# Page buffers, the last pages, transposes and one-hot matrices in a fused graph and expert kernel

## The chip, the cores and the metric

The kernel runs on one NeuronCore of a Trainium2 chip. Its five engines each work through a queue of their own in order: TensorE (PE, with its weight loads PEld), VectorE (DVE), ScalarE (ACT), GpSimd (POOL) and SyncE (SP, which here only issues DMAs). They meet through semaphores. The metric is the device time of one execution in microseconds (us), as the median of several runs.

## The reference, cut to what matters

```python
x = x + agg(layernorm(x)) @ W.T + b          # 12500 nodes, 256 features
#   agg: msgs = features[src] * edge_weight  # 212500 edges, sorted by dst
#        segment_sum(msgs, dst)
h = layernorm(x)
p = softmax(h @ gate_w + gate_b)             # 8 experts
e = argmax(p); pos = rank of the token among the tokens of e, in order
y = relu(h @ w1[e] + b1[e]) @ w2[e] + b2[e]  # 256 -> 1024 -> 256
y = y * p[e] if pos < 1954 else 0            # capacity of an expert
x = x + nan_to_num(y)
```

All of it is float32. One in seventeen of the edges is a node's own loop, the others are random, so the sum over neighbours needs one gathered row of 1 KB for each edge.

## The kernel before, in words

**Edges.** The 212500 edges are cut into 1661 blocks of 128. For a block `k`, `gather(k)` (line 597) is one indirect DMA on POOL that brings 128 rows into the tile `m`; `onehot(k)` (line 605) is one VectorE instruction that makes a 128x128 matrix `h` whose row is the edge's weight at the column of its target; `product(k)` (line 611) multiplies the two on TensorE into the PSUM tile `pw`. Fifteen blocks make a group, after which ScalarE copies `pw` to `ws` (line 619). The pool of `m` has 32 buffers, that of `h` has 12.

**Prologue.** `table()` (line 752) writes the normalised features to `feat` in DRAM, in 14 chunks of eight tiles. Meanwhile the first 112 blocks are gathered from `x` itself and normalised through their weights. In one turn `i` of its loop ScalarE takes statistics of four of the blocks that were gathered (`junk`, lines 772 and 775), scales a chunk (`xn`, line 788), stores it (line 790) and takes a root (`sd`). VectorE takes the other statistics, makes `wr` (line 811) and then, for the eight blocks of turn `i - 2`, one one-hot matrix and one product each (lines 812 to 814). The gathers after the prologue read `feat`, so the first of them waits for the last store.

**Main loop.** From then on one loop (line 826) writes down the order of all engines, step by step: one gather, one scatter or one piece of a page's end, one-hot matrices until `made` is eight blocks ahead of `done` (lines 837 to 839), one product that lies sixteen blocks behind the gather, a piece of `nodes()`, a piece of `experts()`. No scheduler moves anything afterwards.

**Nodes and routing.** `nodes()` (line 622) adds the groups up for each tile of 128 nodes, multiplies by `W`, and for each chunk of eight tiles `route()` (line 244) finds the expert and the place of each token. Its rows go by indirect DMA from POOL (`put`, line 339) to `buf` in DRAM, which holds a page of 128 tokens for each 128 places of an expert. `listing()` (line 360) then finds which pages have become full and writes their numbers to `li`; `SLOTS` (line 49) says how many are taken after each chunk, as pairs of pages at first and as single pages after the last three.

**Pages.** `load()` (line 427) reads a page's number into a register of SP and issues five DMAs there: the page `pg` (line 437), `b1_sb`, `b2_sb`, and the weights `w1_sb` and `w2_sb` of 1 MB each (lines 448 and 450). `pg` has two buffers, the four others have three. `fresh()` (line 454) normalises on VectorE to `xg`, `turn()` (line 461) transposes on TensorE and copies with ScalarE to `gT`, `products()` (line 472) multiplies by `w1` into `ph` (line 481), applies the bias and relu on ScalarE (line 485), and multiplies by `w2` into `py` (line 492). `finish()` (line 498) adds `b2_sb` (line 502), scales on ScalarE (line 505), cleans infinities and adds the page's rows (lines 509 to 518), takes the token numbers out of `pg` (`tok`, line 520), and sends the rows to `out` by indirect DMA on POOL (line 523). `tok` is the last reader of `pg`. In the main loop `experts()` (line 678) holds up to two loaded pages in `ready`, starts a page `LOADED` (20) steps after its load, and spreads it by `PACE`.

**The last pages.** After the loop, `rest()` (line 544) finds the page of each expert that is only partly full (`last()`, line 410), loads and multiplies these eight in a row, with the transposes of the next page between the two products (`between`, line 556), and lists what was left over; here nothing was. A second way of summing the edges (line 860 on) is there for inputs that the first can't hold; with these inputs it isn't entered.

Of the kernel before, what the change touches and what calls it, by code (L numbers as in the profile page):

```python
# [9 lines left out]
F32 = mybir.dt.float32  # L10
# [8 lines left out]
P = 128  # L19
N = 12500  # L20
D = 256
E = 8
# [20 lines left out]
RW = D + 4  # L43
# [8 lines left out]
LEFT = 24  # L52


LEAD = 16
AHEAD = 8
LOADED = 20
PACE = {1: 2.3, 2: 3.0}

# [2 lines left out]
RB = 8  # L62
# [6 lines left out]
KT = (NE + P - 1) // P  # L69
# [23 lines left out]
def gnn_moe_kernel(ctx: ExitStack, tc: tile.TileContext, x, src, dst, ew, wT, gb, gate_w, gate_b,  # L93
# [123 lines left out]
    class Ffn:  # L217
# [209 lines left out]
        def load(self, of, li, i, e=None):  # L427
            p4 = self.p4
            at = li[0:1, 0, i:i + 1] if e is None else li[0:1, e:e + 1]
            row = nc.values_load(at, engines=[mybir.EngineType.SP], min_val=0, max_val=NP_ * P,  # L430
                                 skip_runtime_bounds_check_because="a page, or the empty one")
            if e is None:
                e = nc.values_load(li[0:1, 1, i:i + 1], engines=[mybir.EngineType.SP], min_val=0,
                                   max_val=E - 1,
                                   skip_runtime_bounds_check_because="an expert")
            pg = p4.tile([P, 2, RW], F32, name="pg")
            self.loads.append(nc.sync.dma_start(
                pg[:, :of, :], buf[ds(row, of * P), :].rearrange("(a p) d -> p a d", p=P)))
            return (of, pg) + self.weights(e)
# [95 lines left out]
                send(a)  # L535
                yield 1

        def page(self, of, li, i):
            got = self.load(of, li, i)
            through(self.products(*got, self.turn(got[0], self.fresh(*got[:2]))))  # L540
            through(self.out)


        def rest(self):
            lp = self.last()
            got, turned = {}, {}
            for e in range(2):
                got[e] = self.load(1, lp, 0, e)
            through(self.listing(1, LEFT, count=True))
            news = {0: self.fresh(*got[0][:2])}  # L550
            turned[0] = self.turn(1, news[0])
            for e in range(E):
                if e + 2 < E:
                    got[e + 2] = self.load(1, lp, 0, e + 2)

                def between():
                    if e + 1 < E:
                        turned[e + 1] = self.turn(1, news[e + 1])

                if e + 1 < E:  # L560
                    news[e + 1] = self.fresh(*got[e + 1][:2])
                through(self.products(*got[e], turned[e], between))
                through(self.out)
            left = nc.values_load(left_i, min_val=0, max_val=LEFT,  # L564
                                  skip_runtime_bounds_check_because="a count of pages")
            with tc.If(left > 0):
                self.sends, self.before = [], None
                for i in range(4):
                    self.page(1, self.li, i)
                with tc.If(left > 4):  # L570
                    self.sends = []
                    for i in range(4, LEFT):
                        self.page(1, self.li, i)


    with tc.tile_pool(name="edges", bufs=1) as edges:
# [8 lines left out]
        with tc.tile_pool(name="p2", bufs=32) as p2, tc.tile_pool(name="p2h", bufs=12) as p2h, \  # L585
# [9 lines left out]
            pool_q, pages = [], []  # L595
# [26 lines left out]
            def nodes():  # L622
                xs, shifts = [], {}

                def shift(t):

                    for g in groups_of(t) if t < NT else ():
                        s = p2o.tile([P, P], F32, name="s", bufs=8)
                        nc.vector.tensor_scalar(s, cols, float(P * t), win[:, g:g + 1], op0=ALU.add,  # L629
                                                op1=ALU.is_equal)  # L630
                        shifts[t, g] = s

                for c, (t0, nt, rows) in enumerate(CHUNKS):
                    rt = p3.tile([P, CH, RW], F32, name="rt")
                    ln = ln_new(p3)
                    for t in range(t0, t0 + nt):
                        for i in range(len(xs), min(t + 3, NT)):
                            x_ = p3.tile([P, D], F32, name="xt", bufs=4)
                            r = min(P, N - i * P)
                            nc.scalar.dma_start(x_[:r, :], x[i * P:i * P + r, :])  # L640
                            xs.append(x_)
                        if t == 0:
                            shift(t)
                        gs = groups_of(t)
                        while gs[-1] not in sums:
# [12 lines left out]
                        yield  # L658
                        px = ffn.psum("px")[:, :D]
                        for k in range(2):  # L660
                            nc.tensor.matmul(px[:rows, :], aT[:, k * P:k * P + rows], wT_sb[:, k, :],  # L661
                                             start=(k == 0), stop=(k == 1))
                        x1 = rt[:rows, t - t0, :D]
                        nc.vector.tensor_add(x1, xs[t][:rows, :], px[:rows, :])  # L664
                        nc.vector.tensor_add(x1, x1, gb_sb[:rows, :])
                        ln_stats(ln, x1, t - t0, rows)
                    yield from ffn.route(rt, ln, t0, nt, rows)
                    pool_q.extend(ffn.put)
                    if c < len(CHUNKS) - 1 and SLOTS[c][1]:
                        yield from ffn.listing(*SLOTS[c])  # L670
                        li = ffn.li
                        while pool_q:
                            yield
                        of, n = SLOTS[c]
                        pages.extend((of, li, i) for i in range(n))
                        yield

            def experts(now):
                ready, work, at = [], None, 0.0
                while pages or ready or work:  # L680
                    if pages and len(ready) < 2:
                        ready.append([now[0], ffn.load(*pages.pop(0)), None])
                    if ready and not ready[0][2] and now[0] >= ready[0][0] + LOADED - 3:
                        ready[0][2] = ffn.fresh(*ready[0][1][:2])
                    if not work and ready and now[0] >= max(at, ready[0][0] + LOADED):
                        _, got, xg = ready.pop(0)
                        at = max(at, now[0]) + PACE[got[0]]
                        work = ffn.products(*got, ffn.turn(got[0], xg))
                    elif work and now[0] >= at:
                        at += PACE[got[0]]  # L690
                        if next(work, None) is None:
                            work = None
                            outs.append(ffn.out)
                    yield
# [57 lines left out]
            def table():  # L752
# [3 lines left out]
                for i in range(n + 2):  # L756
# [51 lines left out]
                    if i >= 2:  # L808
                        k0 = (i - 2) * RB
                        wr = p3.tile([P, RB], F32, name="wr")  # L810
                        nc.vector.tensor_mul(wr, w_sb[:, k0:k0 + RB], r[:, CH:])
                        for k in range(k0, k0 + RB):
                            onehot(k, wr[:, k - k0:k - k0 + 1])
# [12 lines left out]
            while alive or pages or b or outs:  # L826
# [33 lines left out]
    with tc.If(some > 0):  # L860
# [49 lines left out]
        with tc.tile_pool(name="q3", bufs=2) as p3, tc.tile_pool(name="q4", bufs=2) as p4, \  # L910
# [6 lines left out]
            for c, (t0, nt, rows) in enumerate(CHUNKS):  # L917
# [25 lines left out]
                if c < len(CHUNKS) - 1 and SLOTS[c][1]:  # L943
                    through(ffn.listing(*SLOTS[c]))
                    for i in range(SLOTS[c][1]):
                        ffn.page(SLOTS[c][0], ffn.li, i)
            ffn.rest()


# [38 lines left out]
```

## Time and profile before

| | us |
|---|---|
| median of 3 runs (2605.55 to 2607.30) | 2607.29 |
| the profiled execution, its own time | 2604.47 |
| its span, first to last instruction | 2602.7 |
| PE, DVE, ACT, POOL busy | 2038.7, 1156.7, 503.9, 1809.1 |
| mean granted clock of TensorE | 0.856 of full |
| gathers from `feat` on POOL, 1549 | 1511.3 busy, 976 ns each |
| DMA | 455.67 MB, 175 GB/s over the span |

Busy time isn't the same as what sets the end: for a stage one looks at which engine waits for nothing there. A line of the timeline has the start, the duration, engine, source line, operation, `output<-inputs`, a count of neighbours of the same kind (x8), and in brackets the idle time of that engine just ahead and what ended it. A line of a table of stretches has, after the length, each engine's busy us and number of instructions, then the granted clock, the busy share of the 16 DMA engines and their GB/s. "SPq" is SP's queue of DMA issues.

### The profile page before, as it was taken

Reading aid. Unit: us, or ns where it says so; the run is one execution under the profiler, and the core shown is the slowest. Engines: PE = TensorE matmul, PEld = TensorE weight load, DVE = VectorE, ACT = ScalarE, POOL = GpSimd, SP = SyncE. Lnnn points to the kernel's source line nnn. Section 1 sums busy time; section 2 is a strip of 40 time slices with the busy share of each in tenths; the row PEclk is TensorE's granted clock in tenths of the full one; section 3 lists DMA queues with packets and bytes.
Section 4 is the critical chain, followed back from the end, with each engine's and each line's share of the span. In section 5 each row is a group of like instructions: output and inputs, shape, how many; then the busy total and the mean of one; then the engine's idle time right before and its main releaser. Section 6 shows DMA issues by size and latency. Waiting matters only on the chain. (4 is left out here: it accounts for less than half of the span.)

```text
span 2602.7 us, 31144 instructions
## 1 busy us (share of the span) xinstructions
PE 2038.7 (78%) x9082; PEld 1619.6 (62%) x9082; DVE 1156.7 (44%) x4287; ACT 503.9 (19%) x1315; POOL 1809.1 (70%) x1859
## 2 busy tenths in 40 slices
PE   2568778887788788788788788788888787788765
PEld 2456545674677576576676676676676565577764
DVE  6875434345336236235335335335335344354322
ACT  5751001111112112112112112112111111122322
POOL 7657777777777777777777777777777777774100
PEclk9668777899789799799889888899898897899978
DMA  8869334544564564564654654654653534677765
GB/s 280 282 205 330 115 107 124 188 150 125 188 185 123 185 186 122 187 184 121 190 182 121 190 183 120 188 182 120 188 183 118 186 109 124 205 246 224 218 185 153
DMA packets 264704, 455.67 MB, mean 175 GB/s; under 512 B 44799, under 2 KB 190406, under 8 KB 264520
## 3 DMA queue, kind: packets, MB, share of 16 engines
q0 software_dynamic: 88800, 240.41, 30.3%
q1 hardware_dynamic: 136210, 174.68, 21.3%
q10 hardware_dynamic: 39510, 38.41, 4.5%
q8 instruction: 81, 1.33, 0.2%
q14 instruction: 103, 0.84, 0.1%
HBM read 387.86 MB, written 67.83 MB: 175 GB/s over the span
## 5 line engine op out<-in xcount | busy, mean ns | idle before, releaser
L599 POOL DMA_INDIRECT m<-feat,src_i x1549 | 1511.3, 976 | 491.0 <-issue 222.4
L616 PE MATMUL pw<-m,h 128*128 128x256 f32 x3322 | 1104.1, 450 | 421.3 <-DMA m<-feat,src_i 294.8
L616 PEld LDWEIGHTS pw<-m,h 128*128 128x128 f32 x3322 | 663.1, 221 | 681.5 <-issue 267.7
L607 DVE TENSOR_SCALAR h<-cols,rel,w_sb 128x128 f32<-128x128 f32 x1549 | 470.4, 357 | 296.6 <-PE pw L616 293.5
L481 PE MATMUL ph<-gT,w_sb 128*128 128x256 f32 (+1 forms) x1856 | 374.6, 355 | 30.7 <-DMA w_sb<-in_w 23.8
L481 PEld LDWEIGHTS ph<-gT,w_sb 128*128 128x128 f32 x1856 | 319.0, 206 | 69.8 <-issue 27.1
L492 PE MATMUL py<-w_sb,hT 128*128 128x256 f32 x1456 | 348.3, 384 | 0.0
L492 PEld LDWEIGHTS py<-w_sb,hT 128*128 128x128 f32 x1456 | 277.1, 193 | 36.6
L485 ACT ACTIVATE hT<-ph,b_sb 128x256 f32<-128x256 f32 (+1 forms) x464 | 168.0, 426 | 510.1 <-PE ph L481 482.2
L523 POOL DMA_INDIRECT out<-z,tok x91 | 90.8, 998 | 189.5 <-DVE tok L520 140.4
L664 DVE TENSOR_TENSOR rt<-xt,ms 128x256 f32<-128x256 f32 x98 | 41.0, 419 | 335.7 <-PE ms L661 335.6
L652 PEld LDWEIGHTS ms<-s,ws 128*128 128x128 f32 x1116 | 175.4, 214 | 18.2 <-DVE s L629 3.1
L652 PE MATMUL ms<-s,ws 128*128 128x128 f32 x1116 | 174.9, 297 | 3.3 <-DVE s L629 3.3
L457 DVE TENSOR_SCALAR xg<-pg 128x256 f32<-128x256 f32 x91 | 35.9, 424 | 298.5 <-DMA pg<-buf 298.5
L619 ACT COPY ws<-pw 128x256 f32<-128x256 f32 x111 | 41.2, 371 | 615.2 <-PE pw L616 615.1
L502 DVE TENSOR_TENSOR y<-py,b_sb 128x512 f32<-128x512 f32 (+1 forms) x58 | 33.4, 576 | 242.8 <-PE py L492 242.8
L599 POOL DMA_INDIRECT m<-in_x,src_i x112 | 107.5, 960 | 46.5 <-issue 22.6
L339 POOL DMA_INDIRECT buf<-rt,to x98 | 98.4, 1004 | 51.7 <-issue 18.6
L661 PE MATMUL ms<-wT_sb,aT 128*128 128x256 f32 x392 | 106.5, 396 | 2.5 <-ACT aT L656 2.4
L505 ACT ACTIVATE y<-y,pg 128x256 f32<-128x256 f32 x91 | 42.7, 503 | 314.0 <-DVE y L502 255.7
L656 ACT COPY aT<-ms 128x256 f32<-128x256 f32 x98 | 36.6, 373 | 261.8 <-PE ms L652 259.5
L661 PEld LDWEIGHTS ms<-wT_sb,aT 128*128 128x128 f32 x392 | 77.3, 199 | 15.4 <-ACT aT L656 4.1
(159 smaller groups left out, 1255.5 us busy)
## 6 DMA issues: line engine op xcount, KB each, us to landing
w_sb<-in_w SPq DMA_DIRECT2D x116, 1024.0 KB, 10.7
m<-feat,src_i POOLq DMA_INDIRECT x1549, 2.8
buf<-fill SPq DMA_DIRECT2D x13, 1300.0 KB
xt<-in_x ACTq DMA_DIRECT2D x97, 128.0 KB, 2.3
xt<-in_x SPq DMA_DIRECT2D x12, 1024.0 KB
feat<-xn ACTq DMA_DIRECT2D x12, 1024.0 KB, 10.6
out<-rt ACTq DMA_DIRECT2D x11, 1024.0 KB, 4.8
pg<-buf SPq DMA_DIRECT2D x33, 260.0 KB, 3.0
```

The source lines that it names most:

```text
L339: s = nc.gpsimd.indirect_dma_start(out=buf[:, :], out_offset=bass.IndirectOffsetOnAxis(ap=to[:, j, :], axis=0), in_=rt[:rows, j, :], in_of ...
L481: nc.tensor.matmul(ph[:, c:c + n], w1_sb[:, k, f * P:(f + 1) * P], xT[:, k * n:(k + 1) * n], start=(k == 0), stop=(k == 1))
L485: nc.scalar.activation(hT[:, f, :n], ph[:, c:c + n], AF.Relu, bias=b1_sb[:, f:f + 1])
L492: nc.tensor.matmul(py[:, a, :], hT[:, f, a * P:(a + 1) * P], w2_sb[:, f, :], start=(f == 0), stop=(f == F // P - 1))
L505: nc.scalar.activation(y[:, a, :], y[:, a, :], AF.Copy, scale=pg[:, a, D + 2:D + 3])
L523: s = nc.gpsimd.indirect_dma_start(out=out[:, :], out_offset=bass.IndirectOffsetOnAxis(ap=to[:, a, :], axis=0), in_=z[:, a, :], in_offset= ...
L599: nc.gpsimd.indirect_dma_start(out=m, out_offset=None, in_=x[:, :] if k < RAW else feat[:, :], in_offset=bass.IndirectOffsetOnAxis(ap=src_ ...
L607: nc.vector.tensor_scalar(h, cols, rel[:, k:k + 1], w_sb[:, k:k + 1] if w is None else w, op0=ALU.is_equal, op1=ALU.mult)
L616: nc.tensor.matmul(product.pw, hs.pop(k), ms.pop(k), start=(j == 0), stop=last)
L619: nc.scalar.copy(ws, product.pw)
L652: nc.tensor.matmul(pa[:, k * P:(k + 1) * P], sums[g][:, k * P:(k + 1) * P], shifts[t, g], start=(g == gs[0]), stop=(g == gs[-1]))
L661: nc.tensor.matmul(px[:rows, :], aT[:, k * P:k * P + rows], wT_sb[:, k, :], start=(k == 0), stop=(k == 1))
```

## The change

Five things are edited. `pg` gets four buffers. `rest()` keeps only the pages that are left over: the eight partly full pages are now found by `nodes()` after the last chunk, with `last()` and the last `listing()`, and join the queue that `experts()` works off. `experts()` keeps a page's transposed rows beside it in `ready`, and hands `between` to `products()`, so that the transposes of the next page, if its `xg` is made, are issued between the two products of the one at work. In the prologue the eight one-hot matrices of a turn are made in reversed order, all ahead of the eight products. In the main loop they are made four at a time (`HB`), in reversed order, when the number that is ahead falls below eight. The other way of summing edges gets the same last pages.

```diff
+HB = 4
@@ load
-            pg = p4.tile([P, 2, RW], F32, name="pg")
+            pg = p4.tile([P, 2, RW], F32, name="pg", bufs=4)
@@ rest
-            lp = self.last()
-            got, turned = {}, {}
-            for e in range(2):
-                got[e] = self.load(1, lp, 0, e)
-            through(self.listing(1, LEFT, count=True))
...
-                through(self.products(*got[e], turned[e], between))
-                through(self.out)
             left = nc.values_load(left_i, min_val=0, max_val=LEFT,
@@ nodes
                     pool_q.extend(ffn.put)
-                    if c < len(CHUNKS) - 1 and SLOTS[c][1]:
-                        yield from ffn.listing(*SLOTS[c])
+                    last = c == len(CHUNKS) - 1
+                    if last or SLOTS[c][1]:
+                        if last:
+                            lp = ffn.last()
+                        yield from ffn.listing(*SLOTS[c] if not last else (1, LEFT, True))
                         li = ffn.li
                         while pool_q:
                             yield
-                        of, n = SLOTS[c]
-                        pages.extend((of, li, i) for i in range(n))
+                        if last:
+                            pages.extend((1, lp, 0, e) for e in range(E))
+                        else:
+                            of, n = SLOTS[c]
+                            pages.extend((of, li, i) for i in range(n))
                         yield
@@ experts
                 ready, work, at = [], None, 0.0
+
+
+                def between():
+                    if ready and ready[0][2] and not ready[0][3]:
+                        ready[0][3] = ffn.turn(ready[0][1][0], ready[0][2])
+
                 while pages or ready or work:
                     if pages and len(ready) < 2:
-                        ready.append([now[0], ffn.load(*pages.pop(0)), None])
+                        ready.append([now[0], ffn.load(*pages.pop(0)), None, None])
...
-                        _, got, xg = ready.pop(0)
+                        _, got, xg, xT = ready.pop(0)
                         at = max(at, now[0]) + PACE[got[0]]
-                        work = ffn.products(*got, ffn.turn(got[0], xg))
+                        work = ffn.products(*got, xT or ffn.turn(got[0], xg), between)
@@ table
-                        for k in range(k0, k0 + RB):
+                        for k in reversed(range(k0, k0 + RB)):
                             onehot(k, wr[:, k - k0:k - k0 + 1])
+                        for k in range(k0, k0 + RB):
                             product(k)
@@ main loop
-                while made < min(KT, max(done, s - LEAD) + AHEAD):
-                    onehot(made)
-                    made += 1
+                if made < min(KT, max(done, s - LEAD) + AHEAD):
+                    for k in reversed(range(made, min(KT, made + HB))):
+                        onehot(k)
+                    made = min(KT, made + HB)
```

More of the change, by code (lines that the diff above doesn't have):

```diff
@@ L536, in finish, with page @@
                 yield 1
-        def page(self, of, li, i):
-            got = self.load(of, li, i)
+        def page(self, *what):
+            got = self.load(*what)
             through(self.products(*got, self.turn(got[0], self.fresh(*got[:2]))))
@@ L544, in rest @@
         def rest(self):
-            lp = self.last()
-            got, turned = {}, {}
-            for e in range(2):
-                got[e] = self.load(1, lp, 0, e)
-            through(self.listing(1, LEFT, count=True))
[L550 to L561, printed above, removed]
-                through(self.products(*got[e], turned[e], between))
-                through(self.out)
             left = nc.values_load(left_i, min_val=0, max_val=LEFT,
@@ L811, in table @@
                         nc.vector.tensor_mul(wr, w_sb[:, k0:k0 + RB], r[:, CH:])
+                        for k in reversed(range(k0, k0 + RB)):
+                            onehot(k, wr[:, k - k0:k - k0 + 1])
                         for k in range(k0, k0 + RB):
-                            onehot(k, wr[:, k - k0:k - k0 + 1])
                             product(k)
@@ L946, in gnn_moe_kernel @@
                         ffn.page(SLOTS[c][0], ffn.li, i)
+            through(ffn.listing(1, LEFT, count=True))
+            lp = ffn.last()
+            for e in range(E):
+                ffn.page(1, lp, 0, e)
             ffn.rest()
```

## The prediction

> **What bounds the kernel now.** I read the busy time by slices first, then cut the span where POOL's behaviour changes, and read each stretch from its timeline.
>
> ```profile
> 0.00:172.70 172.70, 80.39 (x214) 61.09 (x214) 130.27 (x564) 115.89 (x346) 108.69 (x121) 0.78 0.77 251
> 172.70:2374.10 2201.40, 1798.79 (x7896) 1415.73 (x7895) 954.83 (x3446) 325.55 (x779) 1677.04 (x1714) 0.86 0.54 168
> 2374.10:2490.00 115.90, 93.00 (x567) 83.28 (x565) 44.20 (x182) 37.60 (x111) 14.65 (x16) 0.93 0.64 202
> 2490.00:2602.70 112.70, 66.54 (x410) 59.46 (x410) 27.41 (x97) 24.90 (x80) 8.75 (x9) 0.85 0.58 175
> ```
>
> Row 2 is the main loop. POOL's timeline there shows a gather of 0.95 us, 0.30 us of gap and the next gather, 1.25 us a step. From 188 us to the last gather at 2373.17 only one gap is over 0.35 us (0.82, at 1265.83). The loop is therefore POOL's, whatever PE (82% busy) does. Gather k waits for product k-32, issued 16 steps earlier, so PE may fall some 16 steps (20 us) behind before POOL notices.
>
> Row 1, the prologue, ends with the first gather from `feat`:
>
> ```profile
> 143.63 2.14 DVE L607 TENSOR_SCALAR h<-cols,rel,wr 128x128 f32<-128x128 f32 x8
> 144.03 4.21 PE L616 MATMUL pw<-m,h 128*128 128x256 f32 x9 [4.84 <-DVE h L607]
> 144.41 0.22 ACT L183 ACTIVATE sd<-ve 128x16 f32<-128x16 f32 x1 [0.47 <-DVE h L607]
> 146.99 0.37 ACT L619 COPY ws<-pw 128x256 f32<-128x256 f32 x1 [2.36 <-PE pw L616]
> ...
> 172.72 0.94 POOL L599 DMA_INDIRECT m<-feat,src_i  x1 [16.97 <-PE pw L616]
> ```
>
> PE starts when the first of eight one-hot matrices is made; ACT, in order, stands before `ws` until PE has closed a group. The gather at 172.72 names PE, but that product was long done: the last store of `feat` was issued at 168.99, behind ACT's work. Turns without a `ws` copy take ACT 9.24 us (`sd` at 41.42, then 50.66), with no idle time; a turn with one takes that plus the wait (6.20, then 15.8). VectorE in turn waits for `sd` (2.0 to 2.2 us) after most such copies. The chain ACT, DVE, PE, ACT sets the prologue.
>
> Rows 3 and 4, the tail, hold 17 single pages. From PE's timeline, and then DVE's and SP's:
>
> ```profile
> 2477.27 6.72 PE L481 MATMUL ph<-gT,w_sb 128*128 128x128 f32 x32 [3.21 <-DMA w_sb<-in_w]
> 2483.83 3.62 PE L492 MATMUL py<-w_sb,hT 128*128 128x256 f32 x16
> 2492.00 0.20 PE L422 MATMUL ms<-c,page_of 128*1 128x8 f32 x2 [4.54 <-DVE c L420]
> ...
> 2502.05 6.30 PE L481 MATMUL ph<-gT,w_sb 128*128 128x128 f32 x32 [4.49 <-DMA w_sb<-in_w]
> 2508.19 0.38 PE L466 MATMUL pT<-ident,xg 128*128 128x128 f32 x2
> 2508.40 3.62 PE L492 MATMUL py<-w_sb,hT 128*128 128x256 f32 x16
> 2511.86 3.73 PE L481 MATMUL ph<-gT,w_sb 128*128 128x128 f32 x32
> ```
>
> ```profile
> 2515.13 0.15 DVE L520 CAST tok<-pg 128x1 int32<-128x1 f32 x1
> ...
> 2515.41 0.36 SPq L437 DMA_DIRECT2D pg<-buf  x1
> ```
>
> ```profile
> SPq L437 <- DVE tok L520: 720.3, 35, 37.5
> ```
>
> PE waits for weights; the weights are issued 1.4 to 1.9 us after `pg` in SP's order; and `pg`, with two buffers, waits until `tok` of two pages earlier is read. So a load starts only as the page ahead of it starts its first product.
>
> **The Trainium skill.** "DMA: Bandwidth & Descriptors", Anatomy of one DMA: semaphore waits are made by the issuing sequencer, not by the DMA engines; the lines above agree (0.13 us from the end of `tok` to the issue, the weights queued behind). The same page, Specifications, gives some 358 GB/s of HBM for a core; single microseconds of the tail show 382 and 391 GB/s. "TensorE: Matmul & The Clock Gate", Part 1: an idle PE drops to half clock and warms up again; the trace agrees (32 matmuls 3.73 us warm, 6.30 and 6.72 after idling). "SBUF — State Buffer", Who interferes with whom: a VectorE instruction in a two-port mode locks GpSimd out for its length. Partly seen: the gather at 1223.37 took 3.02 us under the unbroken `fin`, `hi`, `z` of a page, and six such gathers cost 11.9 us over 0.95 each; but 60 gathers wholly under one-hot matrices averaged 0.976, against 0.953 for 554 with VectorE idle.
>
> **The change, part by part**, against the span of 2602.7.
>
> *One-hot matrices in the prologue.* PE's first product now waits for the last of eight matrices: 7 x 0.267 (2.14/8) = 1.87 us later. Six `ws` copies lie ahead of the last store (waits 6.20, 4.73, 4.36, 3.13, 2.36, 1.35), none hidden: 6 x 1.87 = **+11.2**. Bound below: 0, if the chain has slack. Above 13.1, a seventh. PE loses seven of eight semaphore waits a burst; I give that nothing, since the bursts are paced by PE's clock.
>
> *One-hot matrices in fours.* The number is the same; DVE now waits on a product two steps behind instead of five, and what stands behind it there (node sums, `xn`, `xg`) may be up to 1.1 us later; its readers on PE come two steps, 2.5 us, later. Covered by POOL. Without the cover, it is 4 x 0.27 = 1.07 us per four steps of PE. **0.**
>
> *Four `pg` buffers in the loop.* The third load of a chunk follows the second at once (weights have three buffers), so about 21 us of full DMA instead of 14, beside the gathers. Before, ten such bursts gave one POOL stall of 0.82. I take **+3**; bounds 0 and +12 (1 us a burst). The meeting of gathers with page ends can shift too: -12 (none of the six) to +54 (all 33 pairs, 27 more at 2 us).
>
> *Transposes between products.* In the tail PE idled for `gT` up to 2.3 us a page; now its copy lies under the second product. In the loop it is nothing (POOL).
>
> *The last pages, and `pg` in the tail.* A load is now held by `b2_sb` (three buffers, free at the y addition of the previous page), 15 us ahead of its use, against some 8 us for 2.37 MB (30.64 MB at 63.3% of 160 us for 13 pages is 7.8 us each of DMA). So PE should set the pitch: 3.83 (product to transposes, at 2556.03) + 0.25 + 3.46 (2508.40 to 2511.86) = 7.54; `xg` follows `finish` of the page before (y addition 2512.06, `tok` done 2515.28, `xg` 0.41), ready about when PE asks: 7.65, against 10.1 before.
> Start: `last()` now stands in PE's order before the fourth tail page. DVE had `to` of the last chunk at 2429.05; its six small instructions take 1.34, so `L424` runs at about 2430.5 and that page starts at 2430.7 instead of 2426.87. PE has idled 6.2 us, and I add 2.7 for the cold clock (6.3 and 6.72 against 3.8) and 0.6 for the listing: next page at 2441.7. Then 13 x 7.65 = 99.5: the last product ends at 2541.1 against 2583.9, **-42.8**. What follows (3.5 us of finish, one send, the end) stays. The 14.6 us hole around 2492 is in this sum. SP's extra wait, for `lp`, is over two pages before its first load is due.
>
> Sum: +11.2 + 3 - 42.8 = -28.6, a span of 2574 and a median of 2607.3 - 28.6 = **2578.7**, 1.1% less. The profiled execution lies 2.8 below the median shown, so 0.1% goes with which run one takes; under 0.2% can't be told from no change.
>
> **Rivals.**
> (B) *The prologue hides it.* If ACT or DVE has slack that the waits don't show, the +11.2 goes: 2567.5. For it: DVE idles 1 to 2 us before `ve` in some turns. Against: ACT doesn't idle otherwise.
> (C) *Weights set the tail.* Two loads overlapping, with the slow row of `b2_sb` (79 and 94 GB/s at 80 to 92% busy for 2 us), may need 9.0 us: 13 x 1.35 = +17.5, 2596. Against: full streams reach 380 GB/s.
> (D) *Slower.* Fours put unbroken VectorE work ahead of `fin`, `hi`, `z`, and more gathers are locked out for 2 us. From 14 more on, of 27 possible pairs, the gain is gone; all 27 give 2633. For it: all six cases had four one-hot matrices just ahead. Against: `fin` waits for ACT's y, which usually opens a gap.
> (E) *The loads stay late* because another wait on SP replaces `pg`: the pitch stays at 10.1, 13 x 2.45 = 31.9 of the gain are lost, 2610.6.
>
> **How the numbers follow.** A 0.55 (own range 2568 to 2588), B 0.17, C 0.14, D 0.08, E 0.06. Leaving out D, E and some 0.05 at the low end gives 2560 to 2600. Faster: A, B, C, 0.86. Same: most of E and a little of D, 0.06. Slower: 0.08.
>
> **What would show it.** Right: first `feat` gather near 184 us; `ws` waits 1.9 longer; gathers still 1.25 apart; last gather near 2387; PE in the tail at 7.6 to 7.8 a page with no wait for weights, a 6 us hole before `last()`'s matmul. Wrong: a first gather at 173 (B), waits for `w_sb` in the tail (C, E), many gathers of 3 us (D).

## The result, and the profile after

| us | before | after |
|---|---|---|
| median | 2607.3 (2605.55 to 2610.18, 4 runs) | 2575.53 (2568.71 to 2578.96, 4 runs) |
| profiled execution, its span | 2604.47, 2602.7 | 2575.36, 2573.6 |
| mean granted clock of TensorE | 0.856 | 0.867 |

The ratio is 0.9874, with a 95% interval of 0.9852 to 0.9896: the change takes 1.3% off. Two later comparisons put it 29.0 and 31.1 us below the kernel before (changed_third and changed_again, among the experiments). The forecast was 2578.7, 3.2 us above the median, and the case with the greatest chance came. Three of its terms were off all the same, and they cancelled. I cut both spans at two events that each kernel has: the first gather from `feat`, and the start of the last full product of a node step (`ms<-wT_sb,aT`, 128x256).

| stretch, us | before | after | difference | forecast |
|---|---|---|---|---|
| prologue, to the first `feat` gather | 172.72 | 182.48 | +9.76 | +11.2 |
| loop, to the last full node product | 2211.29 | 2204.70 | -6.59 | +3 |
| tail, from there to the end | 218.69 | 186.42 | -32.27 | -42.8 |
| span | 2602.7 | 2573.6 | -29.1 | -28.6 |

Of the loop's 6.59 us, 4.37 lie between the first and the last `feat` gather (2200.45 us before, 2196.08 after); the other 2.22 come off what lies between POOL's last gather and the last full node product (10.84 before, 8.62 after).

The table of stretches of the kernel after (columns as in the prediction; the cuts are the first and the last `feat` gather and the start of the even pages):

```profile
0.00:182.48 182.48, 75.57 (x201) 57.49 (x202) 130.55 (x564) 115.79 (x345) 109.26 (x121) 0.77 0.73 238
182.48:2378.56 2196.08, 1815.94 (x7921) 1402.36 (x7920) 977.23 (x3450) 326.63 (x779) 1671.78 (x1713) 0.87 0.54 170
2378.56:2457.00 78.44, 58.36 (x316) 51.01 (x315) 30.57 (x150) 22.45 (x61) 10.74 (x11) 0.83 0.48 155
2457.00:2573.60 116.60, 96.50 (x650) 88.82 (x648) 38.67 (x124) 40.00 (x130) 13.63 (x14) 0.94 0.73 234
```

VectorE, ACT and POOL did the same work as before in the prologue (130.27, 115.89 and 108.69 us busy then) and had 10 us more for it. In the third row PE is busy 74% of the time at a clock of 0.83; in the fourth, 83% at 0.94. So the tail has a poor half and a good half.

*Prologue.* The timeline of the kernel after, at the turn that the prediction showed:

```profile
149.43 2.21 DVE L590 TENSOR_SCALAR h<-cols,rel,wr 128x128 f32<-128x128 f32 x8
151.69 6.14 PE L599 MATMUL pw<-m,h 128*128 128x256 f32 x16 [6.63 <-DVE h L590]
154.65 0.37 ACT L602 COPY ws<-pw 128x256 f32<-128x256 f32 x1 [4.20 <-PE pw L599]
...
182.48 0.95 POOL L582 DMA_INDIRECT m<-feat,src_i  x1 [19.07 <-PE pw L599]
```

PE's first product comes 2.26 us after the first one-hot matrix of the block, where it came 0.40 after it, and ACT waits 4.20 us for `ws` instead of 2.36. The six waits are 7.61, 5.47, 6.17, 4.91, 4.20 and 3.57: longer by 1.41, 0.74, 1.81, 1.78, 1.84 and 2.22, in sum 9.80. That is the whole loss of the prologue.

*Tail.* PE's timeline of the kernel after, three pages beside the last nodes, the wait for the counts, then the even pages:

```profile
2394.76 0.41 PE L468 MATMUL pT<-ident,xg 128*128 128x128 f32 x2 [2.88 <-DVE xg L459]
2395.01 2.88 PE L494 MATMUL py<-w_sb,hT 128*128 128x256 f32 x8
...
2415.41 0.41 PE L468 MATMUL pT<-ident,xg 128*128 128x128 f32 x2 [3.34 <-DVE xg L459]
...
2434.18 0.41 PE L468 MATMUL pT<-ident,xg 128*128 128x128 f32 x2 [2.82 <-DVE rt L264]
...
2445.51 0.20 PE L424 MATMUL ms<-c,page_of 128*1 128x8 f32 x2 [6.05 <-DVE c L422]
...
2464.66 3.73 PE L483 MATMUL ph<-gT,w_sb 128*128 128x128 f32 x32
2468.55 0.41 PE L468 MATMUL pT<-ident,xg 128*128 128x128 f32 x2 [0.15 <-DVE xg L459]
2468.80 3.62 PE L494 MATMUL py<-w_sb,hT 128*128 128x256 f32 x16
2472.25 3.73 PE L483 MATMUL ph<-gT,w_sb 128*128 128x128 f32 x32
```

The even pages are 7.59 us apart (2464.66 to 2472.25), and no wait for weights is left. The 6.05 us hole ahead of the counts is there as forecast. What the forecast lacks are the three waits shown first, of 2.88, 3.34 and 2.82 us: PE stands before the *next* page's transposes, in the middle of a page whose second product could run. (The third bracket names `rt`, which VectorE makes right behind that page's `xg`.) In the kernel before, the second product of the first of these pages followed its first without a wait, 3.57 us after that one's start (2384.98, 2388.55); here it comes 6.86 us after it (2388.15, 2395.01). Eight `py` then take 2.88 us where they take 1.89 warm. The Trainium skill, "TensorE: Matmul & The Clock Gate", Part 1, says that an idle PE falls to half clock; these numbers agree.

Why `xg` is late stands in the timelines of ACT and VectorE, kernel after:

```profile
2390.18 1.14 ACT L487 ACTIVATE hT<-ph,b_sb 128x128 f32<-128x128 f32 x4 [3.05 <-PE ph L483]
2391.34 1.28 ACT L185 ACT_TABLE_LOAD   x1
2392.63 0.20 ACT L185 ACTIVATE sd<-ve 128x4 f32<-128x4 f32 x1
...
2392.87 0.18 DVE L190 RECIPROCAL rs<-sd 128x4 f32<-128x4 f32 x1 [2.69 <-ACT sd L185]
...
2394.21 0.41 DVE L459 TENSOR_SCALAR xg<-pg 128x256 f32<-128x256 f32 x1
```

`xg` stands on VectorE behind the layer norm of the nodes, which waits for ACT's `sd`; `sd` stands on ACT behind half of the page's `hT` and a table load. PE has ended the first product at 2391.9 and stands behind the transposes of `xg`.

On SP the wait for `tok` (in the tail 115.5 us in 14 waits before) gave way to the one that the prediction named, a bias that waits for a `y` (in the tail 37.7 us in 12 waits, with 7.9 left for `tok`). It holds nobody up: in this tail no wait of PE names a DMA. Over the whole run:

```profile
SPq L448 <- DVE y L504: 149.5, 23, 14.3
```

### The profile page after: what moved, and what is told of

Read it like the earlier page. It is cut to its first block, busy times and chain, and to the rows that moved or that the text cites. A ratio compares the mean times of both kernels' runs of the same rounds, so it can differ in the third digit from the quotient of the medians.

```text
span 2573.6 us, 30236 instructions
## 1 busy us (share of the span) xinstructions
PE 2046.4 (80%) x9082; PEld 1599.7 (62%) x9082; DVE 1177.0 (46%) x4287; ACT 504.9 (20%) x1315; POOL 1805.4 (70%) x1859
## 5 line engine op out<-in xcount | busy, mean ns | idle before, releaser
L599 PEld LDWEIGHTS pw<-m,h 128*128 128x128 f32 x3322 | 654.0, 219 | 701.9 <-DMA m<-feat,src_i 406.2
L483 PE MATMUL ph<-gT,w_sb 128*128 128x256 f32 (+1 forms) x1856 | 362.7, 346 | 0.0
L483 PEld LDWEIGHTS ph<-gT,w_sb 128*128 128x128 f32 x1856 | 308.7, 199 | 33.3
```

The costliest lines, as they stand in the source:

```text
L483: nc.tensor.matmul(ph[:, c:c + n], w1_sb[:, k, f * P:(f + 1) * P], xT[:, k * n:(k + 1) * n], start=(k == 0), stop=(k == 1))
L599: nc.tensor.matmul(product.pw, hs.pop(k), ms.pop(k), start=(j == 0), stop=last)
```

## The experiments

Four runs were on a chip of the first comparison's kind; in the other eight, on two chips, the kernel before took 3561.9 and 3578.4 us. There POOL's loop had 121 to 148 gaps of over 0.4 us, 969 to 1010 us in sum, and the engines stood still with no releaser that the profile shows, as PE does here between products of one page (changed kernel with the old prologue):

```profile
1014.30 2.34 PE L494 MATMUL py<-w_sb,hT 128*128 128x256 f32 x5
1019.42 0.38 PE L494 MATMUL py<-w_sb,hT 128*128 128x256 f32 x1 [2.77 <-issue]
1020.86 0.59 PE L494 MATMUL py<-w_sb,hT 128*128 128x256 f32 x1 [1.06 <-issue]
1023.65 0.59 PE L494 MATMUL py<-w_sb,hT 128*128 128x256 f32 x1 [2.20 <-issue]
```

What makes these pauses I can't say. They are in every kernel profiled there. They also reach into the prologue, whose first `feat` gather came at 195.5 to 211.3 us with no relation to its code. So from those runs I use the tails, which hold no such pause and agree with the other chips (the changed kernel's tail takes 188.5 us there, 186.4 and 179.6 elsewhere; with the old prologue it is 187.0 and 186.1, and in the last version below 169.7 and 171.6), and the durations of single instructions. The ratios are given, but a few us in them decide nothing.

| run | median; before it, us | ratio to before (95%) | first `feat` gather | tail: to the counts + from them = all |
|---|---|---|---|---|
| before (first comparison) | 2607.3 | | 172.72 | 107.99 + 110.70 = 218.69 |
| after (first comparison) | 2575.53; 2607.3 | 0.9874 (0.9852 to 0.9896) | 182.48 | 58.33 + 128.09 = 186.42 |
| changed_third | 2573.07; 2602.1 | 0.9889 (0.9874 to 0.9905) | 182.82 | 52.00 + 127.56 = 179.56 |
| old_prologue_again | 2561.61; 2602.1 | 0.9845 (0.9826 to 0.9864) | 172.50 | 58.46 + 127.64 = 186.10 |
| pro_fours | 2567.07; 2602.1 | 0.9869 (0.9851 to 0.9886) | 175.10 | 53.91 + 127.44 = 181.35 |
| best_a_again | 2551.63; 2602.1 | 0.9802 (0.9788 to 0.9815) | 172.24 | 50.08 + 121.53 = 171.61 |
| old_prologue | 3545.29; 3561.9 | 0.9963 (0.9945 to 0.9982) | 209.31 | 59.98 + 127.06 = 187.04 |
| no_between | 3541.26; 3561.9 | 0.9942 (0.9922 to 0.9963) | 208.35 | 47.39 + 140.49 = 187.88 |
| pg_two | 3569.04; 3561.9 | 1.0022 (1.0007 to 1.0037) | 207.72 | 56.56 + 165.28 = 221.84 |
| singles | 3542.98; 3561.9 | 0.9937 (0.992 to 0.9955) | 195.46 | 58.03 + 127.84 = 185.87 |
| changed_again | 3547.3; 3578.4 | 0.9902 (0.9867 to 0.9936) | 200.78 | 61.28 + 127.24 = 188.52 |
| best_a | 3538.3; 3578.4 | 0.9876 (0.9835 to 0.9917) | 210.68 | 48.20 + 121.52 = 169.72 |
| rest_kept | 3567.34; 3578.4 | 0.9959 (0.9936 to 0.9983) | 211.27 | 103.15 + 90.24 = 193.39 |
| pg_alone | 3564.68; 3578.4 | 0.9957 (0.9942 to 0.9973) | 210.16 | 99.47 + 91.34 = 190.81 |

"The counts" is the matmul of `last()`; before, in rest_kept and in pg_alone eight pages follow it, in the others thirteen or fourteen. Seven profiles have the tail of the changed kernel (after, changed_third, changed_again, both old prologues, pro_fours and singles). It varies there by 9 us, 179.6 to 188.5, and nearly all of that lies ahead of the counts: 52.0 to 61.3 us there, 127.1 to 128.1 from the counts on. PE's clock falls and recovers in that first part: in changed_third, after and changed_again its mean granted clock was 0.91, 0.81 and 0.75 there, for 52.0, 58.3 and 61.3 us. So a difference of a few us between two tails, one profile each, is not much of a witness.

**The prologue**

The changed kernel with the prologue of before, on the two kinds of chip, and with its one-hot matrices in fours:

```diff
-                        for k in reversed(range(k0, k0 + RB)):
-                            onehot(k, wr[:, k - k0:k - k0 + 1])
                         for k in range(k0, k0 + RB):
+                            onehot(k, wr[:, k - k0:k - k0 + 1])
                             product(k)
```

> The changed kernel with the one-hot matrices of the prologue again made one by one ahead of their products. Theory (the chain ACT, DVE, PE, ACT carries the prologue, and the reversed eight put 9.8 us on it): the first gather from feat goes from 182.5 back to about 172.7 us, nothing else moves, and the whole is 9 to 11 us shorter than the changed kernel, about 2566. Rival (the prologue is late because of something else in the change): first gather stays at 182 us, no change in the whole.

> The changed kernel with the prologue of the kernel before. Theory (PE's first product of a block waits for the last of eight one-hots made in reverse order, 1.87 us, six or more times on the chain): 9 to 11 us below the changed kernel, time from the first one-hot of a block to its first product 0.4 us instead of 2.2. Rival (the shared engines of the prologue hide it, and the 9.8 us that the first comparison showed there came from something else): within 3 us of the changed kernel, the first gather of feat no earlier.

```diff
-                        for k in reversed(range(k0, k0 + RB)):
-                            onehot(k, wr[:, k - k0:k - k0 + 1])
-                        for k in range(k0, k0 + RB):
-                            product(k)
+                        for q in range(k0, k0 + RB, 4):
+                            for k in reversed(range(q, q + 4)):
+                                onehot(k, wr[:, k - k0:k - k0 + 1])
+                            for k in range(q, q + 4):
+                                product(k)
```

> The changed kernel with the prologue's one-hots in fours, each four made in reverse order and used before the next four. Theory: the first product of a block waits for four one-hots (4 x 0.267 = 1.07 us) instead of eight (2.14), so half of the prologue's loss comes back, 4 to 6 us below the changed kernel, first one-hot to first product 1.2 us. Rival (order of making them is not what counts): within 2 us of the changed kernel.

> The changed kernel without an edit, the yardstick of this call. Both theories: 28 to 33 us below the kernel before; from the last full node product to the end 186 to 189 us, as in its two profiles so far (186.4 and 188.5).

The first run of the old prologue decides nothing: its ratio lies above those of no_between and singles, which have the new prologue, and its first gather at 209.3 us where three kernels with the new prologue have theirs (207.7, 208.4, 211.3). The second one does. Timeline of old_prologue_again, then of pro_fours:

```profile
143.62 2.14 DVE L590 TENSOR_SCALAR h<-cols,rel,wr 128x128 f32<-128x128 f32 x8
144.03 6.00 PE L599 MATMUL pw<-m,h 128*128 128x256 f32 x16 [4.85 <-DVE h L590]
146.99 0.37 ACT L602 COPY ws<-pw 128x256 f32<-128x256 f32 x1 [2.40 <-PE pw L599]
...
172.50 0.95 POOL L582 DMA_INDIRECT m<-feat,src_i  x1 [16.75 <-PE pw L599]
```

```profile
144.91 2.14 DVE L590 TENSOR_SCALAR h<-cols,rel,wr 128x128 f32<-128x128 f32 x8
146.08 6.39 PE L599 MATMUL pw<-m,h 128*128 128x256 f32 x16 [6.45 <-DVE h L590]
149.05 0.37 ACT L602 COPY ws<-pw 128x256 f32<-128x256 f32 x1 [3.12 <-PE pw L599]
...
175.10 0.94 POOL L582 DMA_INDIRECT m<-feat,src_i  x1 [17.29 <-PE pw L599]
```

First one-hot to first product: 0.41 us, 1.17 in fours, 2.26 with all eight. The first gather follows: 172.5, 175.1, 182.8. The medians are 11.5 and 6.0 us below changed_third, the changed kernel run beside them; the interval of the old prologue's ratio lies clear of changed_third's, that of pro_fours overlaps it. (The tail of changed_third, 179.6 us, was expected at 186 to 189.) The loss is the order of eight, it is on the chain, and nothing hides it. In fours less is left of it (2.6 us) than half: six waits of 0.76 would be 4.6.

**Four buffers for pages**

Two again in the changed kernel, and four alone in the kernel before:

```diff
-            pg = p4.tile([P, 2, RW], F32, name="pg", bufs=4)
+            pg = p4.tile([P, 2, RW], F32, name="pg", bufs=2)
```

> The changed kernel with two buffers for pg again. Theory (the page's buffer held the weights back): the tail goes back from 7.6 to about 10 us a page, with waits for w_sb on PE, 12 to 13 pages x 2.5 = 30 us slower than the changed kernel, about 2605. Rival (the joined queue of pages gave the gain, and b2_sb holds the loads back about as late anyway): within 10 us of the changed kernel.

```diff
-            pg = p4.tile([P, 2, RW], F32, name="pg")
+            pg = p4.tile([P, 2, RW], F32, name="pg", bufs=4)
```

> The kernel before with four buffers for pages, and nothing else. Theory (with two, each load of weights stands on SP behind a load of a page that waits for a buffer; that set the 10.1 us between pages): the five pages of the tail ahead of the last eight go from 10.1 to some 8.7 us, the last eight to 7.6, the hole ahead of them stays: some 25 us below the kernel before (2582 where it takes 2607). Rival (another load on SP, that of the biases, or PE's wait for transposes takes the place at once): within 5 us of the kernel before, pages still about 10 us apart.

> The changed kernel again without an edit, so that the three others of this call have it beside them on the same chip. Both theories: 28 to 33 us below the kernel before (2575.5 against 2607.3 in the first comparison), first gather of feat at 182 us, last pages 7.6 us apart.

With two, PE's timeline in the tail and SP's waits (pg_two):

```profile
3452.45 3.81 PE L483 MATMUL ph<-gT,w_sb 128*128 128x128 f32 x32 [2.29 <-DMA w_sb<-in_w]
3457.28 0.41 PE L468 MATMUL pT<-ident,xg 128*128 128x128 f32 x2 [1.02 <-DVE xg L459]
...
3463.15 3.81 PE L483 MATMUL ph<-gT,w_sb 128*128 128x128 f32 x32 [2.01 <-DMA w_sb<-in_w]
```

```profile
SPq L439 <- DVE tok L522: 1000.6, 37, 54.7
```

The wait for `tok` is back (the line is of the whole run with its pauses; in the tail it is 147.2 us in 16 waits), with it the wait for weights and a pitch of 10.7 us, 10.8 in the mean of the last twelve. In time, pg_two is 24 to 28 us above the three kernels run beside it (old_prologue, no_between and singles, each with four buffers and one edit of its own), near the 30 expected. The tail takes 221.8 us, more than the 218.7 of before: without the buffers, the rest of the change does the tail no good. With four buffers in the kernel before, pg_alone:

```profile
3430.95 3.84 PE L481 MATMUL ph<-gT,w_sb 128*128 128x128 f32 x32 [1.14 <-ACT gT L469]
...
3439.61 3.84 PE L481 MATMUL ph<-gT,w_sb 128*128 128x128 f32 x32 [1.14 <-ACT gT L469]
...
3488.86 3.73 PE L481 MATMUL ph<-gT,w_sb 128*128 128x128 f32 x32
...
3496.45 3.73 PE L481 MATMUL ph<-gT,w_sb 128*128 128x128 f32 x32
```

8.66 us a page (3430.95 to 3439.61) where the transposes stand between pages, 7.59 in the last eight, where `rest()` already had them between products. The tail falls by 27.9 us (218.69 to 190.81), close to the 25 expected; the time fell by 13.7 only, on a chip with a thousand us of pauses in the loop, and where the other half went there stays open, since no profile of the kernel before was taken on that chip. So one argument of one tile gives 27.9 us of tail by itself, where the whole change gives 30.2 to 39.1 over the seven profiles, 32.3 in the first comparison.

**Transposes between products**

```diff
-                        work = ffn.products(*got, xT or ffn.turn(got[0], xg), between)
+                        work = ffn.products(*got, xT or ffn.turn(got[0], xg))
```

> The changed kernel with the transposes of a page again issued after the products of the page before it. Theory: the first three pages of the tail lose their waits for xg (2.88, 3.34 and 2.82 us) with the cold clock behind them, some 10 to 12 us less together, and the later pages get a wait for gT of about 1.15 us each, 13 x 1.15 = 15 us more: between 0 and 6 us slower than the changed kernel, the loop unchanged. Rival (the transposes between products are a plain gain in the tail): 13 to 16 us slower, with no gain in the first three pages.

PE's timeline in the tail:

```profile
3412.95 3.84 PE L483 MATMUL ph<-gT,w_sb 128*128 128x128 f32 x32 [1.15 <-ACT gT L471]
...
3421.61 3.84 PE L483 MATMUL ph<-gT,w_sb 128*128 128x128 f32 x32 [1.14 <-ACT gT L471]
```

Each page of the even part waits 1.15 us for `gT` and the pitch is 8.66: from the counts to the end 140.5 us instead of 127.1 to 128.1. But ahead of the counts the three waits for `xg` are gone, and that part takes 47.4 us instead of 52.0 to 61.3. The sum, 187.9 us, is within the 179.6 to 188.5 of the seven, and 0.8 and 2.0 above the two with the same tail run beside it (old_prologue and singles). As they were placed, the transposes between products took some 13 us off one half of the tail and put 5 to 14 on the other.

**The last pages in the common steps**

The changed kernel with the last eight pages in a routine of their own, as before; all else stays:

```diff
         def rest(self):
+            lp = self.last()
+            got, turned = {}, {}
+            for e in range(2):
+                got[e] = self.load(1, lp, 0, e)
+            through(self.listing(1, LEFT, count=True))
...
-                    last = c == len(CHUNKS) - 1
-                    if last or SLOTS[c][1]:
...
+                    if c < len(CHUNKS) - 1 and SLOTS[c][1]:
+                        yield from ffn.listing(*SLOTS[c])
```

> The changed kernel with the last eight pages in a routine of their own after all else, as in the kernel before; four buffers, fours and transposes between products are kept. Theory (the tail's gain is the pitch of the pages, and running the last pages through the common steps gives only the hole of some 15 us ahead of them, of which it gives back 6 us as the wait for the counts and some as waits for xg): 3 to 7 us above the changed kernel, pitch of the last eight 7.6 us. Rival (that the last pages run beside the last nodes is the gain): 20 us or more above the changed kernel, the tail at about 220 us.

The tail is 193.4 us, 4.9 above that of changed_again, run beside it, as the theory has it, and 4.9 to 13.8 above the seven profiles; the rival's 220 is excluded. That the common steps shorten the tail is thus seen, but not by how much. The median is 20.0 above, which is what the rival said, and the profiled execution 12.2, of which 10.5 lie ahead of the first gather, in the part that the pauses disturb; so the time itself is no witness here. What the common steps gain is the long hole ahead of the eight pages (from the counts at 3477.16 to the next product at 3487.16 in rest_kept); what they cost is the wait of 6 us for the counts while pages are still to do.

**One-hot matrices one at a time in the loop**

```diff
-HB = 4
+HB = 1
```

> The changed kernel with HB = 1, one-hot matrices in the main loop made one at a time. Theory (POOL sets the loop, the order of VectorE doesn't): from the first gather from feat to the last gather 2196 us within 6, and the whole within 6 us of the changed kernel, though VectorE waits less for products. Rival (fours keep page ends from locking out gathers): gathers of 2.8 us and more are back, six of them, and the loop is 4 to 8 us longer. Second rival (fours cost semaphore time): the loop is shorter by 10 us or more.

The ratio, 0.9937, is no worse than those of its neighbours, but in the trace something returns. In the kernel before, six gathers of the loop took 2.79 to 3.05 us each, as this one:

```profile
1223.37 3.02 POOL L599 DMA_INDIRECT m<-feat,src_i  x1 [0.30 <-issue]
1223.62 0.41 DVE L509 TENSOR_SCALAR fin<-y 128x512 uint8<-128x512 f32 x1
```

Timeline of singles, at the same point of a chunk:

```profile
1107.44 3.04 POOL L341 DMA_INDIRECT buf<-rt,to  x1 [0.30 <-issue]
1107.67 0.41 DVE L511 TENSOR_SCALAR fin<-y 128x512 uint8<-128x512 f32 x1
1108.00 0.41 DVE L513 TENSOR_SCALAR hi<-y 128x512 f32<-128x512 f32 x1
1108.34 0.41 DVE L516 TENSOR_SCALAR z<-y 128x512 f32<-128x512 f32 x1
...
1109.64 0.73 DVE L519 COPY_PREDICATED z<-fin,y 128x512 f32<-128x512 uint8 x1
```

A POOL instruction (here a scatter into `buf`) that starts just ahead of a page's `fin`, `hi`, `z` isn't done until they and what follows them, up to `COPY_PREDICATED`, are: the scatter ends at 1110.48, `COPY_PREDICATED` at 1110.37. That fits the Trainium skill, "SBUF — State Buffer", Who interferes with whom, which names `tensor_scalar` (`fin`, `hi` and `z` here) among the instructions that can lock GpSimd out in a two-port mode; no run here shows in which mode they ran. Singles has six of them, of 3.04 or 3.05 us; pg_alone, the other kernel here without fours, has six as well, of 3.05; the eleven profiles with fours have none over 2.5 once the loop is under way. The kernel after, at that point of a chunk:

```profile
1231.48 0.40 DVE L511 TENSOR_SCALAR fin<-y 128x512 uint8<-128x512 f32 x1
1231.75 1.63 POOL L582 DMA_INDIRECT m<-feat,src_i  x1 [0.30 <-issue]
1231.81 0.41 DVE L513 TENSOR_SCALAR hi<-y 128x512 f32<-128x512 f32 x1
```

Here the gather starts 0.27 us after `fin`, where before it started 0.25 ahead of it (the scatter of singles 0.23), and takes 1.63. Between the first and the last `feat` gather POOL is busy for 1660.5 us in singles and 1659.2 in pg_alone, against 1652.8 to 1657.2 in the six with fours on those chips; on the other kind of chip 1676.1 before against 1669.3 to 1672.3 in the five with fours. So fours save POOL 3 to 7 us of work on the same kind of chip. The rival's six long instructions are back; whether the loop is 4 to 8 us longer can't be read among the pauses. That fours do it by shifting the end of a page against POOL's beat is how the lines read; no run shifted it by other means. With two `pg` buffers and fours POOL is busy for 1657.2 us, with four (old_prologue, no_between) for 1653.3 and 1653.6; and on the undisturbed chips POOL idles for 524.3 us of this stretch before and 524.3 after. Four buffers cost POOL nothing that is seen.

**Together: a version that is faster than both**

Old prologue; transposes between products only once the node steps are done; the matmul of `last()` sent six steps later:

```diff
-        def last(self):
+        def last(self, steps=0):
...
+            for _ in range(steps):
+                yield
...
-                            lp = ffn.last()
+                            lp = yield from ffn.last(6)
...
-                    if ready and ready[0][2] and not ready[0][3]:
+                    if not alive and ready and ready[0][2] and not ready[0][3]:
...
-                        for k in reversed(range(k0, k0 + RB)):
-                            onehot(k, wr[:, k - k0:k - k0 + 1])
                         for k in range(k0, k0 + RB):
+                            onehot(k, wr[:, k - k0:k - k0 + 1])
```

> The changed kernel with three edits: the prologue makes and uses its one-hot matrices one by one, as before; a page's transposes go between the products of the page ahead only once the node steps are done; the matmul that sums the counts for the last pages is sent six steps later. Theory (what the change gives away is 9.8 us in the prologue, some 11 us of transposes on PE waiting for xg in the first three pages of the tail with the slow clock after them, and the 6.05 us hole ahead of that matmul): some 25 to 30 us below the changed kernel (about 2547 where it takes 2575), no wait for xg over 1.5 us in the tail, hole under 2 us, last eight pages still 7.6 us apart. Rival (those waits only cover others: PE would wait for aT, xT or the gathers instead): no more than the prologue's 10 us below the changed kernel.

> The same three edits as in the run best_a, in more rounds, because there the two ratios (0.9876 and 0.9902) could not be told apart although the tail was 18.8 us shorter. Theory (tail and prologue are separate and what they give back stays): 18 to 20 us below the changed kernel from the tail, and 10 more from the prologue where the loop and the prologue run without pauses of another origin. Rival (the loop or the prologue takes it back): within 5 us of the changed kernel, tail again at 170 us.

The first run left it open in time (0.9876 against 0.9902, with intervals that overlap), though its tail was 18.8 us shorter, 13.1 of it ahead of the counts and 5.7 after them. The second decides: 2551.63 us against 2573.07, 21.4 below the changed kernel, and 0.9802 (0.9788 to 0.9815) of before. PE's timeline there:

```profile
2422.77 3.84 PE L485 MATMUL ph<-gT,w_sb 128*128 128x128 f32 x32 [2.30 <-ACT gT L473]
2426.45 1.89 PE L496 MATMUL py<-w_sb,hT 128*128 128x256 f32 x8
2428.27 0.20 PE L426 MATMUL ms<-c,page_of 128*1 128x8 f32 x2
...
2433.48 3.84 PE L485 MATMUL ph<-gT,w_sb 128*128 128x128 f32 x32 [0.81 <-ACT gT L473]
```

The hole is gone: the counts' matmul waits for nothing. A wait of 2.30 us for `gT` stands one product ahead of it, as in the kernel before (at 2426.87). Against changed_third's profile the prologue is 10.6 us shorter, the tail 8.0 (that profile had the shortest of the changed kernel's three tails, and was the fastest of its runs; against the first one's it is 14.8), and the loop 3.8 longer, with POOL busy 3.0 longer (against the first one's loop it is 1.3). So the 28 to 30 us of my theory were not all had, and "within 5 us" is excluded. Whether the loop's 3.8 us are more than the spread between profiles, and whether they come of the transposes that no longer stand between products there, wasn't tried by itself.

## Why the prediction was right, and where it was not

*The prologue, +11.2.* Right in mechanism: PE waits for the last of eight, the `ws` copies of ACT behind it, and none of it is hidden (rival B falls: undone, 11.5 us come back). The size was 9.8 in the profile, since the first two of six waits grew by 1.41 and 0.74 and not by 1.87.

*Fours, 0.* This step failed. "Covered by POOL" was right for their lateness, but I took the fours' place among VectorE's work as a possible cost alone (rival D) and costed it at nothing. The six gathers of 3 us, which I had seen and summed to 11.9 us, went away. I had bounded such a shift below at -12 and put it under the buffers; the runs put it under the fours: they are there in all three kernels without fours (two buffers before, four in singles and pg_alone), and in none with fours (two buffers in pg_two). Of the 6.6 us that the loop lost, 4.4 lie up to POOL's last gather; POOL's busy time fell by 4.3 there and its idle time not at all. The other 2.2 lie behind that gather, and no run shows what they come of.

*Four `pg` buffers in the loop, +3.* Nothing of it is seen: a stall would be idle time of POOL, and that is 524.3 us in both kernels; nor is POOL busy for longer with four than with two.

*The tail, -42.8.* The mechanism held: the wait for `tok` went, no wait for weights came (C and E fall), the pitch was 7.59 for a forecast of 7.65, the hole 6.05 for 6.2. From the counts to the end of the last product I had 110.6 us (2430.5 to 2541.1); it was 109.8 (2445.51 to 2555.31). The missing 10.5 us lies ahead of it: "`L424` runs at about 2430.5" is 46.5 us after the last full product, and it took 58.3 (52.0 to 61.3 in the seven profiles), 11.8 too many, of which 1.3 came back later. The step that failed is the one on transposes between products. I gave them a gain in the even pages only, and "in the loop it is nothing (POOL)" left out the three pages after POOL's last gather that still run beside the nodes. There PE stands in order behind a transpose whose `xg` is late. The run without them took 47.4 us for this part, so the forecast of 46.5 fits a kernel without this edit.

*Which part earned the gain.* I gave the tail to buffers, transposes and common steps together. The runs part them only in part. The buffers are shown from both sides: alone they give 27.9 us, and without them the tail is as long as before (221.8). The common steps give 4.9 us against the run beside them, the transposes as placed 0.8 to 2.0, and both figures are within the spread of the tail's first part. Each figure is of another kernel, and they need not add up.

The miss of 0.5 us in the sum is thus luck: -1.4 in the prologue, -9.6 in the loop (3 for a cost that didn't come, 4.4 of POOL's work, 2.2 open), +10.5 in the tail.

## What to carry to other kernels

Before moving work between two products on an in-order engine, look at what produces its operand in *each* stage where the code runs, not only in the stage that it is for: here it gains 1.1 us a page in one and loses 5 to 14 us over three pages in the other. A wait on an issuing queue (here SP before a small load) holds back the large loads queued behind it, and two more buffers were worth more here (27.9 us of tail) than the reordering. And making all operands of a burst ahead of it is free only where nobody waits for the first result: in the prologue it cost 9.8 us.

## What I had not expected of the hardware

- The order of the one-hot matrices on VectorE decides how long POOL's own instructions take at the end of a page: one at a time, six of them take about 3.0 us; in fours none does, 3 to 7 us of POOL's time in all.
- PE idle for 3 us can cost more than 3 us, and not always the same. After the first such wait eight `py` took 2.88, 3.22 and 3.62 us in the three profiles of the changed kernel, against 1.89 warm; after the third, of 2.82 us in each, they took 1.89, 1.89 and 3.01. The part of the tail with three such waits took from 52.0 to 61.3 us in these profiles, the part without them from 127.2 to 128.1.
- On two of the chips one thousand us of pauses, which no line of the profile explains, lay over the loop of every kernel profiled there, while their tails lay within 2 us of those elsewhere for two kernels out of three and, for the changed kernel, at 188.5 us against 186.4 and 179.6.
